# A transformer kernel on one core: splitting the first load, moving key preparation, and spreading the entering tiles' work over rounds and queues

## The chip, the cores and the metric

The kernel runs on one core of a Trainium2 chip. The core has five engines that run side by side, each in the order of its own instruction list: TensorE (PE, matrix products and transposes), VectorE (DVE), ScalarE (ACT), GpSimd (POOL) and SyncE (SP), which here only issues transfers. ScalarE and GpSimd issue transfers as well. The metric is the device time of one execution in microseconds, as the median of several runs; lower is better.

## The reference

The input x has 4 batches of 1024 rows and 256 features. Two blocks follow each other, each with an attention over a context and a network behind it; everything is fp32.

```python
x = x + _L0_xattn_ref(_layernorm(x), ctx, ctx, mask, ...)   # 16 heads, 64 masked context keys
x = x + _L0_ffn_ref(_layernorm(x), ...)     # self-attention, gate, norm, 8 experts
x = x + _L1_xattn_ref(_layernorm(x), ctx, ctx, ...)         # 16 heads, no mask
x = x + _L1_ffn_ref(_layernorm(x), ...)     # 8 experts, each takes its 512 best rows
```

`_L0_ffn_ref` is the largest part: queries, keys and values from the normalised rows, scores over all 1024 rows of a batch for 16 heads, scaled by a factor that comes from each query (`sigmoid(q . scale_w) * 2`), softmax, a sigmoid gate, a projection, a layer norm, then one of 8 experts for each row (the larger index of the two best), and a layer norm.

## The kernel before, in words

The 4096 rows are 32 tiles of 128 rows, 8 to a batch; all of x stays on the chip in `xres`. The stages stand one behind the other: cross-attention 0 (to about 260 us), self-attention (to 1307), routing and the experts of the first block (to 1540), cross-attention 1, and the last network.

**Cross-attention** (`cross_attention`, L295) works in rounds. In round r, a list `steps` names what is done, and for which tile: ("share", 5) means that in round r tile r - 5 gets its step `share`. The list also sets the order within the round. While a set `in_order` holds an engine, the instructions that are made through `matmul`, `on_dve`, `on_act`, `on_pool` or `on_sync` stay in program order on it; otherwise the scheduler places them. Before the first round stands `cross_keys` (L259): it loads the weights `xw` and makes the keys of the whole context, `k_t`. `prepare(b)` makes batch b's keys, values and limits (from the mask) in round b, ahead of the round's steps.

In the same rounds runs `beside` (L1447): in round 4 it calls `Entrance.prepare` (scaled query weights and other constants), and from round 27 on (`FIRST_IN`) it lets the 8 tiles of the first batch enter self-attention. The class `Enter` (L552) has the steps of an entering tile: `stats`, `norm`, `turn` (transpose), `keys`, `values`, `queries`, `scale`, `gain`, and `spread`. Keys and queries are split by `halves` (L547) on GpSimd into a rounded part and the rest, by two instructions (L549, L550), into the tiles `kst` and `qst`. `kst` has a single buffer, which holds two tiles. After each second tile `spread` (L610) issues eight transfers of 64 KB that lay these keys out for the heads in `k_rows` (L618). The Entrance also loads three rows (`gb_half`, `n1g`, `last`) by ScalarE's queue as soon as it is made.

**Self-attention** (L623) works in units of 512 queries and 4 heads. `Unit.spread` (L664) lays out a unit's queries by four transfers of 128 KB (L670); `first` makes scores to find each query's largest (`tops`, L694 on VectorE), `second` makes them again, and takes the exponential on ScalarE. The other batches' tiles enter during this stage, by `enter` (L638). The two pools of the stage, sa1 and sa2, take over the memory of pools that are closed by then; a pool without `reuse_waits="tile"` waits for all of what lay there, one with it only for the tiles that it overlaps.

**Routing and experts** (L976): from the counts of the routing, a chain of small VectorE instructions (all shown as L1007, the helper `v`) makes the list of slots, `slot_i` and `slot_row_i`. SyncE reads these (L1053, L1064) to choose the weights and the rows `x_s` that it loads (L1057, L1065). The second block's keys, `k_t` of layer 1, are made by `cross_keys` ahead of this chain, and the batches' keys and values by `meanwhile` behind it.

The instructions that the prediction names by line: L412 is `share`, L401 `lower`, L324 the limits, L392 and L393 `tops` of cross-attention, L408 and L409 `sums`, L442 `bias`, L445 `add`, L598 the tanh of `scale`, L603 `gain`, L269 the eviction of `k_t`. L123 and L126 are the helpers of all products and transposes.

Of the kernel before, what the change touches and what calls it, by code (L numbers as in the profile page):

```python
# [68 lines left out]
def two_blocks(  # L69
# [106 lines left out]
    nc.sync.dma_start(out=xres[:, 0:TB], in_=x_v[:, 0:TB])  # L176
# [20 lines left out]
    def on_all(pool, first, n, queue, width=D):  # L197

        at = ROWS.index(first) * D
        t = new(pool, [P, n, width], f"row_{first}")  # L200
        queue.dma_start(
            out=t.rearrange("p n d -> p (n d)"), in_=rows[at : at + n * width].partition_broadcast(P)
        )
        return [t[:, i] for i in range(n)]
# [54 lines left out]
    def cross_keys(one, layer, xw, queue):  # L259

        bk = cols_sb[:, 4 * layer + 2 : 4 * layer + 4]
# [3 lines left out]
        k_t = new(one, [P, 2, B * SK], f"k_t{layer}")  # L265
        for m in range(2):
            ps = bank()
            product(ps[:, : B * SK], ws[1][:, :, m * P : (m + 1) * P], ctx_sb)
            nc.vector.tensor_scalar(k_t[:, m], ps[:, : B * SK], bk[:, m : m + 1], None, ALU.add)  # L269
        return ws, k_t, *on_all(one, f"bo{layer}", 2, queue)  # L270
# [24 lines left out]
    def cross_attention(layer, ws, k_t, bo, bv, prepared=None, beside=None):  # L295
# [4 lines left out]
        with tc.tile_pool(name=f"xb{layer}", bufs=2) as work:  # L300
# [176 lines left out]
            for r in range(NT + last + (layer == 0)):  # L477
                if r < NT:
                    tiles_of[r] = Tile(r)
                if r < B:  # L480
                    prepare(r)
                for name, behind in steps:
                    if r - behind in tiles_of:
                        getattr(tiles_of[r - behind], name)()
                if beside is not None:
# [23 lines left out]
    class Entrance:  # L509


        def __init__(self, even, pool):
# [6 lines left out]
            self.gb_half = new(pool, [P, 2], "gb_half")  # L519
            at = ROWS.index("gb") * D  # L520
            nc.scalar.dma_start(out=self.gb_half, in_=rows[at : at + D].rearrange("(m p) -> p m", p=P))
            self.n1g, self.n1b = on_all(pool, "n1g", 2, nc.scalar)
            (self.moe_gb,) = on_all(pool, "last", 1, nc.scalar, E)
# [28 lines left out]
    class Enter:  # L552
# [22 lines left out]
        def keys(self):  # L575
            i = self.i
            if i % 2 == 0:
                self.b["kst"] = new(self.ent.pool, [P, 2, 2, 2 * P], "kst", F32R, bufs=1)
            k_f = new(self.work, [P, 2, P], "en_f", bufs=3)
            on_act(nc.scalar.copy(k_f, by_feature(w_k, self.xn_t)))  # L580
            halves(self.b["kst"][:, :, :, i % 2 * P : (i % 2 + 1) * P], k_f)
# [19 lines left out]
        def gain(self):  # L601
            th = self.th
            on_dve(nc.vector.scalar_tensor_tensor(th, th, 1.0, self.q_f, ALU.add, ALU.mult))  # L603
            self.b["gained"] += 1
# [3 lines left out]
            halves(self.b["q"][half][:, :, :, at : at + P], th)  # L608

        def spread(self):  # L610
# [3 lines left out]
            if i % 2 == 0:  # L614
                return
            for g in range(4):
                for half in range(2):
                    nc.sync.dma_start(  # L618
# [936 lines left out]
```

## Time and profile before

| | us |
|---|---|
| median of 3 runs | 2011.66 (2010.49 to 2013.72) |
| the profiled execution's own time | 2024.04 |
| its span | 2022.3 |
| PE busy | 1803.0 (89%) |
| DVE busy | 1409.4 (70%) |
| ACT busy | 1055.6 (52%) |
| POOL busy | 842.3 (42%) |

The busy shares are means over stages with different limits. The chain of waits goes back from the last instruction, at each step to what released it, so its shares say what the time was spent on. In the answers, "idle before" in brackets is the idle time of the engine ahead of an instruction, with what ended it. SPq and ACTq are transfers being issued by SyncE and ScalarE. A wait for several things is put down to the one that came last.

### The profile page before, as it was taken

Reading aid. Unit: us, or ns where it says so; the run is one execution under the profiler, and the core shown is the slowest. Engines: PE = TensorE matmul, PEld = TensorE weight load, DVE = VectorE, ACT = ScalarE, POOL = GpSimd, SP = SyncE. Lnnn points to the kernel's source line nnn. Section 1 sums busy time; section 2 is a strip of 40 time slices with the busy share of each in tenths; the row PEclk is TensorE's granted clock in tenths of the full one; section 3 lists DMA queues with packets and bytes.
Section 4 is the critical chain, followed back from the end, with each engine's and each line's share of the span. In section 5 each row is a group of like instructions: output and inputs, shape, how many; then the busy total and the mean of one; then the engine's idle time right before and its main releaser. Section 6 shows DMA issues by size and latency. Waiting matters only on the chain.

```text
span 2022.3 us, 36959 instructions
## 1 busy us (share of the span) xinstructions
PE 1803.0 (89%) x13599; PEld 1079.3 (53%) x13599; DVE 1409.4 (70%) x2970; ACT 1055.6 (52%) x2201; POOL 842.3 (42%) x1262
## 2 busy tenths in 40 slices
PE   6998779999999999999999999969996888837998
PEld 4666644355455454554544444446664666624566
DVE  6998477877777778777787878266775887854232
ACT  2666416666666666666666666613333666601111
POOL 4888531022232322222322202126667888704443
PEclk8999879999999999999999999979997999957999
DMA  9995120010110101110101100058883311103442
GB/s 276 223 224 119 28 63 22 22 33 22 32 33 22 43 22 26 34 27 22 43 19 51 33 17 1 11 189 253 258 276 95 123 62 57 57 11 84 109 97 36
DMA packets 143443, 160.62 MB, mean 79 GB/s; under 512 B 24976, under 2 KB 116624, under 8 KB 143264
## 3 DMA queue, kind: packets, MB, share of 16 engines
q1 hardware_dynamic: 123552, 128.33, 24.6%
q0 software_dynamic: 9216, 16.93, 3.7%
q10 hardware_dynamic: 10496, 13.01, 1.9%
q8 instruction: 108, 1.77, 0.4%
q14 instruction: 71, 0.58, 0.1%
HBM read 77.33 MB, written 55.72 MB: 66 GB/s over the span
## 4 chain that ended last, share of the span: by engine, by line
PE 62%; DVE 18%; POOL 10%; issue 4%; DMA 3%; ACT 1%; SPq 1%; another core or an unknown queue 0%; POOLq 0%; ACTq 0%; DVEq 0%
PE bank L123 35%; PE acc L123 12%; PE two_banks L123 8%; DVE tops L694 5%; PE bank L126 5%; POOL pr L412 3%; PE first L123 3%; POOL rstd L221 2%; DMA x_s<-xs_d 2%; DVE w_sum L408 2%; DVE mx L393 1%; DVE pr L392 1%; POOL y L248 1%; DVE bn_st L218 1%; DVE xres L442 1%
## 5 line engine op out<-in xcount | busy, mean ns | idle before, releaser
L694 DVE TENSOR_REDUCE tops<-first 128x1 f32<-128x512 f32 x1002 | 644.5, 684 | 218.6 <-PE first L123 180.1
L726 ACT ACTIVATE e<-bank 128x512 f32<-128x512 f32 x1024 | 555.3, 595 | 330.4 <-PE bank L123 309.4
L123 PE MATMUL first<-k_rows,q_rows 32*128 32x512 f32 x2004 | 412.3, 452 | 40.1 <-DVE tops L694 33.2
L123 PE MATMUL bank<-q_rows,k_rows 32*128 32x512 f32 x2048 | 408.8, 451 | 2.3 <-ACT e L726 1.9
L123 PEld LDWEIGHTS bank<-q_rows,k_rows 32*128 32x128 f32 x2048 | 175.6, 184 | 263.9 <-issue 136.5
L123 PE MATMUL acc<-e,vals 128*32 128x512 f32 x2048 | 285.6, 611 | 0.0
L123 PE MATMUL bank<-m_rows,ones_r 32*128 32x512 f32 x1024 | 220.4, 393 | 0.0
L123 PEld LDWEIGHTS first<-k_rows,q_rows 32*128 32x128 f32 x2004 | 169.6, 186 | 77.5 <-DVE tops L694 66.2
L220 POOL TENSOR_SCALAR rstd<-mv 128x1 f32<-128x1 f32 x206 | 49.8, 242 | 338.9 <-DVE mv L219 329.3
L412 POOL TENSOR_TENSOR pr<-pr,w_sum 128x1024 f32<-128x1024 f32 x64 | 126.3, 1974 | 8.2 <-DVE w_sum L409 6.3
L221 POOL TENSOR_TENSOR rstd<-rstd,mhalf 128x1 f32<-128x1 f32 x206 | 121.9, 592 | 17.2
L420 ACT COPY pr_t<-two_banks 128x1024 f32<-128x1024 f32 x64 | 64.8, 1012 | 118.0 <-PE two_banks L126 118.0
L123 PEld LDWEIGHTS bank<-m_rows,ones_r 32*128 32x128 f32 x1024 | 112.6, 185 | 14.1
L123 PE MATMUL two_banks<-xg_t,ew 128*128 128x512 f32 (+1 forms) x288 | 113.1, 551 | 0.0
L549 POOL CAST qst<-en_th 128x256 fp32r<-128x256 f32 x32 | 13.3, 417 | 215.3 <-DVE en_th L603 215.3
L126 PE MATMUL two_banks<-ident,pr 128*128 128x128 f32 x512 | 72.3, 286 | 29.2 <-POOL pr L412 28.9
L123 PEld LDWEIGHTS acc<-e,vals 128*32 128x32 f32 x2048 | 42.7, 108 | 102.1 <-issue 92.6
L1385 ACT ACTIVATE h_t<-two_banks 128x512 f32<-128x512 f32 (+1 forms) x36 | 19.8, 550 | 145.1 <-PE two_banks L123 145.1
L254 POOL DMA_INDIRECT out_x<-y,tok_i x32 | 50.4, 1574 | 98.9 <-DVE y L1213 91.9
L126 PEld LDWEIGHTS two_banks<-ident,pr 128*128 128x128 f32 x512 | 58.1, 145 | 51.2 <-POOL pr L412 50.1
L1386 DVE TENSOR_TENSOR h_t<-h_t,two_banks 128x512 f32<-128x512 f32 (+1 forms) x36 | 22.6, 628 | 89.1 <-ACT h_t L1385 84.3
L123 PE MATMUL bank<-xw,o_t 128*128 128x256 f32 x256 | 71.0, 400 | 14.1 <-ACT q_t L366 11.1
(287 smaller groups left out, 3413.5 us busy)
## 6 DMA issues: line engine op xcount, KB each, us to landing
w_s<-in_w SPq DMA_DIRECT2D x78, 512.0 KB, 5.3
xs_d<-zeros SPq DMA_DIRECT2D x8, 4112.0 KB, 53.2
q_rows<-qst SPq DMA_DIRECT2D x128, 128.0 KB, 2.4
k_rows<-kst SPq DMA_DIRECT2D x128, 64.0 KB, 2.0
ew<-in_e SPq DMA_DIRECT2D x15, 512.0 KB, 3.9
x_s<-xs_d SPq DMA_DIRECT2D x39, 128.5 KB, 4.1
ys_d<-y ACTq DMA_DIRECT2D x39, 128.0 KB, 3.5
ew<-in_e ACTq DMA_DIRECT2D x9, 512.0 KB, 5.8
```

The costliest lines, as they stand in the source:

```text
L123: return placed(nc.tensor, nc.tensor.matmul(*args, **kw))
L126: return placed(nc.tensor, nc.tensor.transpose(*args))
L218: on_dve(nc.vector.bn_stats(st, src))
L220: on_pool(nc.gpsimd.tensor_scalar(r, mv[:, 1:2], EPS, None, ALU.add))
L221: on_pool(nc.gpsimd.tensor_tensor(r, r, mhalf, ALU.pow))
L254: return nc.gpsimd.indirect_dma_start(out=dst[:], out_offset=bass.IndirectOffsetOnAxis(ap=idx, axis=0), in_=src[:], in_offset=None, comput ...
L408: on_dve(nc.vector.tensor_reduce(self.w, self.pr, AX.X, ALU.add))
L412: on_pool(nc.gpsimd.tensor_tensor(self.pr, self.pr, self.w.unsqueeze(2).to_broadcast(bc), ALU.mult))
L420: on_act(nc.scalar.copy(self.pr_t.rearrange("p j q -> p (j q)"), tp))
L694: nc.vector.tensor_reduce(self.part[:, i, j, at : at + 1], self.ps[j], AX.X, ALU.max)
L726: nc.scalar.activation(self.es[k][:, j], ps, AF.Exp)
L1386: on_dve(nc.vector.tensor_tensor(h, h, ps[:, CAP : CAP + n], ALU.mult))
```

## The change

1. The load of the first batch of x is issued in two parts, tiles 0 and 1, then 2 to 7.
2. `cross_keys` is divided: `cross_weights` loads, and a new `cross_keys` makes `k_t`, with its eviction in VectorE's program order. For layer 0 it is called in round 0 behind the steps. For layer 1 it is called in `meanwhile`, behind the chain that makes the slots.
3. `prepare(r)` is called behind the steps of its round. The Entrance's three row loads are issued in round 2 (in ScalarE's order), and `Entrance.prepare` runs in round 6.
4. For the tiles of the first batch, the key split and `spread` come one round later than the keys, and the query split one round later than `gain`; the key copy has buffers of its own (`en_k`). The cross-attention has one more round for this.
5. Of the last pair's eight key transfers, four are issued by SyncE and four by ScalarE. The first unit's four query transfers are issued by ScalarE.
6. The pools sa1 and sa2 get `reuse_waits="tile"`.

On the engines the lists stay the same but for these moves: TensorE's order differs only by the batches' value products in the first rounds.

```diff
-    nc.sync.dma_start(out=xres[:, 0:TB], in_=x_v[:, 0:TB])
+    for first, end in (0, 2), (2, TB):
+        nc.sync.dma_start(out=xres[:, first:end], in_=x_v[:, first:end])
...
-    def cross_keys(one, layer, xw, queue):
-
-        bk = cols_sb[:, 4 * layer + 2 : 4 * layer + 4]
+    def cross_weights(one, layer, xw, queue):
+
         w = new(one, [P, 2, 4 * D], f"xw{layer}")
         queue.dma_start(out=w, in_=xw.rearrange("(c p) n -> p c n", p=P))
         ws = [w[:, :, i * D : (i + 1) * D] for i in range(4)]
-        k_t = new(one, [P, 2, B * SK], f"k_t{layer}")
+        return ws, new(one, [P, 2, B * SK], f"k_t{layer}"), *on_all(one, f"bo{layer}", 2, queue)
+
+    def cross_keys(layer, ws, k_t):
+        bk = cols_sb[:, 4 * layer + 2 : 4 * layer + 4]
         for m in range(2):
             ps = bank()
             product(ps[:, : B * SK], ws[1][:, :, m * P : (m + 1) * P], ctx_sb)
-            nc.vector.tensor_scalar(k_t[:, m], ps[:, : B * SK], bk[:, m : m + 1], None, ALU.add)
-        return ws, k_t, *on_all(one, f"bo{layer}", 2, queue)
+            on_dve(nc.vector.tensor_scalar(k_t[:, m], ps[:, : B * SK], bk[:, m : m + 1], None, ALU.add))
...
-            for r in range(NT + last + (layer == 0)):
+            for r in range(NT + last + 2 * (layer == 0)):
                 if r < NT:
                     tiles_of[r] = Tile(r)
-                if r < B:
-                    prepare(r)
                 for name, behind in steps:
                     if r - behind in tiles_of:
                         getattr(tiles_of[r - behind], name)()
+                if r == 0 and layer == 0:
+                    cross_keys(0, ws, k_t)
+                if r < B:
+                    prepare(r)
...
         def keys(self):
+            self.k_f = new(self.work, [P, 2, P], "en_k" if self.on_scalar else "en_f", bufs=2 if self.on_scalar else 3)
+            on_act(nc.scalar.copy(self.k_f, by_feature(w_k, self.xn_t)))
+
+        def split_keys(self):
             i = self.i
             if i % 2 == 0:
                 self.b["kst"] = new(self.ent.pool, [P, 2, 2, 2 * P], "kst", F32R, bufs=1)
-            k_f = new(self.work, [P, 2, P], "en_f", bufs=3)
-            on_act(nc.scalar.copy(k_f, by_feature(w_k, self.xn_t)))
-            halves(self.b["kst"][:, :, :, i % 2 * P : (i % 2 + 1) * P], k_f)
+            halves(self.b["kst"][:, :, :, i % 2 * P : (i % 2 + 1) * P], self.k_f)
...
+            queues = (nc.sync, nc.scalar) if self.on_scalar and i == TB - 1 else (nc.sync, nc.sync)
             for g in range(4):
                 for half in range(2):
-                    nc.sync.dma_start(
+                    placed(
+                        queues[half],
+                        queues[half].dma_start(
...
-        with tc.tile_pool(name="sa1", bufs=1) as one, tc.tile_pool(name="sa2", bufs=2) as work:
+        with (
+            tc.tile_pool(name="sa1", bufs=1, reuse_waits="tile") as one,
+            tc.tile_pool(name="sa2", bufs=2, reuse_waits="tile") as work,
+        ):
...
+                    queue = nc.scalar if self.first_of_all else nc.sync
                     for half in range(2):
                         for r in range(2):
-                            nc.sync.dma_start(
+                            queue.dma_start(
...
-            enter_steps += ("spread", 3), ("scale", 4), ("gain", 4)
+
+            enter_steps += ("scale", 4), ("gain", 4), ("split_keys", 4), ("spread", 4), ("split_queries", 5)
 
             def beside(work, r):
 
-                if r == 4:
+                if r == 2:
+                    ent.load()
+                if r == 6:
                     ent.prepare()
...
     def meanwhile():
+        cross_keys(1, *keys_1[:2])
         prepared.extend(keys_of_batch(xa1, 1, *keys_1[:2], keys_1[3], b) for b in range(B))
```

`ent.load` is the new home of the three row loads (in ScalarE's order); `split_queries` holds the two lines of `gain` that took the query split.

## The prediction

> **What bounds the kernel now.** I read the page first, then the chain of waits by windows, then the timeline at the three places that the edit touches: the first 45 us, the end of the first cross-attention (190 to 265 us), and the step from self-attention to the routed layer (1325 to 1345 us).
>
> ```profile
> span 2022.3 us, 36959 instructions
> PE 62%; DVE 18%; POOL 10%; issue 4%; DMA 3%; ACT 1%; SPq 1%; another core or an unknown queue 0%; POOLq 0%; ACTq 0%; DVEq 0%
> ```
>
> TensorE carries 62% of the chain, but none of the edited places is limited by TensorE: there the chain is on VectorE, GpSimd, SyncE's queue and loads. So a microsecond saved at these places is a microsecond of the span, as long as what follows is in series. It is: self-attention can't start before all keys of the first batch have landed, and the routed layer can't before routing.
>
> Start, from the timeline (start, duration, what, and in brackets the idle time before it):
>
> ```profile
> 16.07 1.28 ACT L350 ACT_TABLE_LOAD   x1 [16.07 <-DMA row_n1g<-in_rows]
> ...
> 19.51 0.69 PE L126 MATMUL bank<-ident,xn 128*128 128x128 f32 x2 [3.38 <-ACT xn L350]
> 20.00 0.43 DVE L324 TENSOR_SCALAR lim<-lim 128x512 f32<-128x512 int32 x1 [0.30 <-DMA lim<-in_mask]
> ...
> 29.15 1.22 DVE L392 TENSOR_TENSOR pr<-two_banks,lim 128x1024 f32<-128x1024 f32 x1
> ```
>
> ScalarE does nothing until 16.07, because three row loads (gb_half, n1g, last) stand in its queue. VectorE, from 45 to 165 us the busiest engine (117.75 of 120 us), does its first score row at 29.15.
>
> The ring of the entering tiles, from the chain of waits (start, duration, what):
>
> ```profile
> 213.59 1.09 PE two_banks L126 x8
> 214.68 1.06 PE two_banks L123 x8
> 215.74 0.37 PE bank L126 x2
> 216.11 3.11 PE bank L123 x24
> ...
> 220.63 0.74 POOL qst L550
> 221.37 1.87 POOL pr L412
> ...
> 253.58 0.74 POOL kst L550
> ...
> 260.60 2.46 DMA q_rows<-qst
> ...
> 263.19 0.76 PE first L123
> ```
>
> Read the first six as a circle: the shares (L412) feed the transposes, these are followed in TensorE's order by the entering tile's products; tanh, gain and the first half of the query split (219.25 to 220.56) are left out; its second half (L550) stands before the next L412 in GpSimd's order. L412 starts at 192.13, 201.94, 211.63, 221.32, 231.29, 241.45: 9.7 to 10.2 us a round, against 5.6 us before. The last three show the exit: key split done at 254.32, then 12 issues in SyncE's queue (8 keys, 4 queries), the last starting at 260.60, and its landing.
>
> Routing, from the timeline:
>
> ```profile
> 1330.85 0.48 DVE L269 TENSOR_SCALAR k_t<-bank,cols_sb 128x256 f32<-128x256 f32 x1 [1.21 <-PE bank L123]
> ...
> 1332.53 0.48 DVE L269 TENSOR_SCALAR k_t<-bank,cols_sb 128x256 f32<-128x256 f32 x1 [1.20 <-PE bank L123]
> 1332.93 0.16 DVE L1007 TENSOR_TENSOR total<-next_row,region 128x8 f32<-128x8 f32 x1
> ```
>
> VectorE ends place_i at 1329.63 and then waits for TensorE's layer 1 keys, while the routing (total, and from it slot_i, for which SyncE's queue waits) stands behind.
>
> **The change part by part.** The sum is made on the profiled execution: span 2022.3, its own time 2024.04, which is 12.4 above the median of 2011.66. I take the difference over to the median unscaled, since the edited stretches are short.
>
> *Start.* Two issues instead of one for x (0.44 us each on SyncE, which waits for its own loads anyway) let tile 0 arrive with a quarter of the bytes. Its statistics move ahead of the keys, and the masks' and keys' preparation of each batch behind the round's steps. Tile 0's chain then ends when GpSimd's setup does (12.4) plus rstd, power, shift, xn (0.31+0.61+0.26+0.60 with gaps: 15.0), and the transposes follow the first values' product at about 15.0 instead of 19.51. The following rounds do the same VectorE work: keys, values, limits 2.2 us, statistics 0.6. Limits of batch 1 still wait for a load (20.00 before, perhaps 19.4 with 256 KB of n1g gone from ahead). Counted on from there: limits 1 end at 20.4, statistics 2 at 21, batch 2 at 24, tops of tile 0 start at 24.6 (29.15 before); but batch 3's 2.2 us now lie behind these, so that tops of tile 1 start at 29.7 against 32.10. That is 2.4 us, kept by a VectorE that is full from there on. The scaling of w_q and its two neighbours (4 us on VectorE) moves from round 4 to 6, paid in both. The three row loads cost ScalarE 0.37+0.35+0.35 us at round 2; the transfers before them in its queue are over by then. Ends: 0.5 us, if limits 2 and 3 are as late as the loads let them be; 4.6, if all of the 29.15 to 24.6 is kept. I take 2.4, since the 2.2 us of batch 3 are paid anyhow.
>
> *Entering.* Key split, key transfers and query split go one round later, so the ring opens. What is late next is a longer circle: gain (VectorE), the next round's tops 2.45, sums with reciprocal 1.46, bias and add about 1.6, statistics 0.6, then GpSimd's rs 1.3, both splits 2.26, L412 1.9. Counted on by these rows, with L412 at 184.54 unchanged, the next start at 191.0 (no key split in that round), 198.8, 210.5, 219.0 and 228.5. The last of these in full: TensorE's transposes after 210.5 + 1.9, its products 5.55 (1.07+0.37+3.11 and the transposes' 1.0), tanh and gain 0.85 end at 218.8; + 2.45 + 1.46 + 1.6 + 0.6 on VectorE is 224.9, + 1.3 + 2.26 on GpSimd is 228.5. Then comes a new wait: there is one buffer for two tiles' split keys, so a pair's first split waits for the previous pair's landings. Pair 1's split ends at 227.4, its last issue starts 7 x 0.635 later (231.8) and lands after 2.0: 233.9. GpSimd waits there, and shares, lower and everything behind it with it. Two splits 2.26: L412 of the last tile at 236.2, against 241.45. So of the 9.7 us rounds only 5.2 us are won in five. At the end the same wait returns: pair 2's split ends at 239.2, lands at 245.8, then key, query, key splits (3.4) end at 249.3 against 254.32.
>
> *Two queues.* The last eight key transfers go four and four; ScalarE then issues the four queries. But ScalarE is in order, and ahead stand the last two tanh. The last follows TensorE's last keys by 3.4 us, as before (252.56 to 255.97): 251.0 if TensorE runs the last rounds as now, 249.5 at full clock. Eight issues, seven intervals of 0.635, then 2.46 to landing and 0.14: TensorE's first complete products at 258.0 or 256.5 against 263.19. So entering and queues together give 5.2 to 6.7; I take 5.5, nearer the present clock (0.83 in the rounds of 221 to 251 us). The other queries' issues stay on SyncE and come earlier; ScalarE's next work, a copy at 277.34, is far. The lifted pool waits (reuse by tile) hide behind these transfers: GpSimd's memset waited for the query split until 258.21, but what needs it comes in the next batch; without this cover they would be worth no more than the 0.6 us from 258.15 to 258.74. Ends for this part: 1.5 (only the issues saved less the wait for tanh) and 9.
>
> The Trainium skill's page "DMA: Bandwidth & Descriptors", section "Issuing engines are not separate DMA queues", speaks against the two queues: all queues run on the same 16 engines, and a second issuing engine saves only the sequencer's time, "usually small relative to the DMA itself". The rows show 12 issues taking 7.6 us against 2.46 for a landing, so here the small part is the large one. Were the page right on the size, this part would give under 1 us and the sum would be about 10 instead of 11.2.
>
> *Routing.* The two k_t evictions go behind the routing's chain on VectorE (pos ends at 1341.95 before), so total starts at 1329.65 instead of 1332.93: 3.3 us earlier, and slot_i, SyncE's loads and x_s with it. In the way: the scatters into xs_d (last issue ends 1335.47; transfers run to about 1337) are over when x_s would now be issued (1337.2). TensorE's last two value products wait for the evictions' banks (1339.6) and end about 1340.6, before slot 0's transposes (1344.45 - 3.3 = 1341.1). The evictions' 0.96 us delay the layer 1 keys, which are needed in 200 us. Ends: 1.0 (scatters or banks hold x_s) and 3.3. I take 3.3.
>
> Sum: 2.4 + 5.5 + 3.3 = 11.2 us. 2011.66 - 11.2 = 2000.5 (profiled: 2024.0 - 11.2 = 2012.8).
>
> **The rivals.**
> 1. *All three as summed*: 2000.5, with 1992.7 (4.6+9+3.3, and 2 for the clock) to 2006. For it: each of the waits is printed with its releaser.
> 2. *The key buffer takes the place of the ring.* If landing takes a microsecond or two longer than the 2.0 measured, the wait on pairs 1 and 2 eats the 5.2 us and the entering gives 1.5. Then 2011.66 - 2.4 - 1.5 - 3.3 = 2004.5. For it: the wait is really added; against: DMA share is 0.06 to 0.16 in these rounds.
> 3. *Hidden anyway.* The start stays at the pace of its loads (0.5), x_s waits for scatters (1.0), entering 1.5: 3.0 us, 2008.7, which is within 0.2%.
> 4. *Slower: the wait on landings becomes the bound.* GpSimd now waits three times (pairs 0, 1, 2) for eight landings with the whole softmax queued behind. The far row is the load of x at 12.4 us to landing: three times 10.4 more gives 2000.5 + 31 = 2031.7. It decides from 5 us more each (11.2 + 4 = 15). Against it: the queues are nearly empty there.
>
> **How the numbers follow.** Chances: 0.62, 0.18, 0.11, 0.09. 0.2% (4 us) is about what a measurement of this kernel can tell from no change. Cases 1 and 2 are faster (0.80), with 0.01 of case 3 above the bound; case 3 leaves 0.10 as the same; case 4 0.09 slower. Predicted is case 1. The range reaches over cases 1 to 3: below to 1992.7, the sum of the upper ends (17) with 2 for a half-clock spell of 3.4 us more or less; above to 2009.
>
> **What would show it.** Right: the first table load of ScalarE near 4 us, the first tops near 24.6; L412 of the last tile near 234 (236 less the start's 2.4), the key splits of tiles 4 and 6 released by a DMA; eight issues between the last tanh and the first products, these about 8 us earlier in the span; total directly after place_i, and slot 0's transposes 11 us earlier. Wrong: an L412 period still near 9.7 with no DMA wait, ScalarE held at its three row loads at round 2, or slot 0 waiting for scatters.

## The result, and the profile after

The changed kernel takes 2008.63 us against 2014.57 us for the kernel before (medians of 19 runs each on the same chip); the ratio is 0.9975 with a 95% interval of 0.9967 to 0.9983, which is 5.0 us less (3.4 to 6.6). The forecast was 11.2 us less. The time lay inside the range given, but less than half of the gain came.

The profiled execution of the changed kernel took 2008.63 us, its span is 2006.9. The profiled execution of before, on which the prediction was built, took 2024.04, which is 9.5 above the median of its 19 runs: from the first score row of self-attention to the start of the last place_i (the routing's result, where each row goes) it needs 1065.5 us, and 1052.6 to 1059.1 in the sixteen other profiles of this case, with and without the change; why is not known. So the two spans must not be subtracted; the places are compared one by one. The page's chain of waits reaches back over the last tenth of the span only and then breaks off:

```profile
span 2006.9 us, 36970 instructions
...
PE 9%; DVE 2%; issue 1%; POOL 0%; DMA 0%; POOLq 0%; ACT 0%; ACTq 0%; DVEq 0%
```

So all that follows is read from timelines. In this kernel's lines L417 is `share`, L406 `lower`, L397 `tops`, L282 the keys and L293 the clearing of the values' buffer, L275 the eviction of `k_t`, L558 and L559 the splits, L609 the tanh.

The start, from the timeline of the changed kernel (start, duration, what, idle time before it):

```profile
4.82 1.28 ACT L355 ACT_TABLE_LOAD   x1 [4.82 <-DMA ctx_sb<-in_ctx_t]
...
25.42 1.23 DVE L397 TENSOR_TENSOR pr<-two_banks,lim 128x1024 f32<-128x1024 f32 x1
...
27.81 2.45 DVE L282 TENSOR_TENSOR keys<-k_t,head 128x256 f32<-128x256 f32 x2
...
27.98 2.01 POOL L406 TENSOR_TENSOR pr<-pr,mx 128x1024 f32<-128x1024 f32 x1 [1.28 <-DVE mx L398]
...
32.36 1.23 DVE L397 TENSOR_TENSOR pr<-two_banks,lim 128x1024 f32<-128x1024 f32 x1
```

ScalarE is free at 4.82 instead of 16.07, and the first tops start at 25.42 instead of 29.15, both near the forecast. But the two keys of batch 3, 0.73 us in the other rounds, now run while GpSimd works on `lower`, and take 2.45. Tile 1's tops start at 32.36; they started at 32.10 before. Nothing is left of the lead. The same place in the timeline of before, where L277 are the keys, L392 `tops`, and L526 and L527 are of `Entrance.prepare`:

```profile
25.12 0.72 DVE L277 TENSOR_TENSOR keys<-k_t,head 128x256 f32<-128x256 f32 x2
...
32.10 1.19 DVE L392 TENSOR_TENSOR pr<-two_banks,lim 128x1024 f32<-128x1024 f32 x1
...
36.75 1.94 POOL L526 MEMSET vals<- 128x2208 f32 x1
37.01 1.95 DVE L527 TENSOR_SCALAR wq<-fw_sb 128x512 f32<-128x512 f32 x1
```

The last two lines stood in the profile from which the prediction was made: a 128x512 `tensor_scalar`, which takes 0.43 us for the limits, took 1.95 beside a `memset` of GpSimd. The prediction counted it in its "4 us on VectorE" without asking why it was so long.

The last rounds of the entering tiles and the exit, from the same timeline:

```profile
229.28 1.90 POOL L417 TENSOR_TENSOR pr<-pr,w_sum 128x1024 f32<-128x1024 f32 x1
...
234.26 0.40 POOL L558 CAST kst<-en_k 128x256 fp32r<-128x256 f32 x1 [3.07 <-ACT en_x_t L239]
...
236.56 1.91 POOL L417 TENSOR_TENSOR pr<-pr,w_sum 128x1024 f32<-128x1024 f32 x1
...
245.73 0.40 POOL L558 CAST kst<-en_k 128x256 fp32r<-128x256 f32 x1 [4.76 <-DMA k_rows<-kst]
...
248.50 0.73 POOL L559 TENSOR_TENSOR kst<-en_k,kst 128x256 fp32r<-128x256 f32 x1
...
249.91 0.38 ACT L609 ACTIVATE en_th<-bank 128x256 f32<-128x256 f32 x1 [0.33 <-PE bank L123]
249.99 2.46 ACTq L635 DMA_DIRECT2D k_rows<-kst  x4
...
252.49 2.57 ACTq L694 DMA_DIRECT2D q_rows<-qst  x4
...
257.83 0.76 PE L123 MATMUL first<-k_rows,q_rows 32*128 32x512 f32 x1 [0.87 <-DMA q_rows<-qst]
```

All of this is as forecast: shares at 229.28 and 236.56 (forecast 228.5 and 236.2), GpSimd's two new waits for the key buffer, key splits done at 249.23 (249.3), then the last tanh, eight issues of ScalarE, and the first complete products at 257.83 instead of 263.19. (The first of the two waits is put down to ScalarE's `en_x_t`, which came last. That it was the key buffer shows in the kernel with two of them, below: there the wait is gone.)

Routing, from the same timeline, and the row of SyncE's waits there (engine, line, what it waited for: us in total, times, longest):

```profile
1314.01 0.17 DVE L902 CAST place_i<-place 128x4 int32<-128x4 f32 x1
1314.09 0.16 DVE L1031 TENSOR_TENSOR total<-next_row,region 128x8 f32<-128x8 f32 x1
...
1317.69 3.26 SPq L1081 DMA_DIRECT2D w_s<-in_w  x3
...
1319.06 1.18 POOL L258 DMA_INDIRECT xs_d<-xr,place_i  x1 [0.30 <-issue]
...
1323.55 2.73 PE L123 MATMUL bank<-xw,ctx_sb 128*64 128x256 f32 x16 [4.16 <-DVE k_t L275]
...
1324.39 0.36 SPq L1089 DMA_DIRECT2D x_s<-xs_d  x1
...
1326.66 0.66 PE L126 MATMUL bank<-ident,x_s 128*128 128x128 f32 x2 [0.38 <-DMA x_s<-xs_d]
```

```profile
SPq L1089 <- DMA xs_d<-xr,place_i: 2.4, 2, 1.3
```

The same in the timeline of before, where place_i starts at 1329.46:

```profile
1336.61 2.81 SPq L1057 DMA_DIRECT2D w_s<-in_w  x3
...
1340.49 0.36 SPq L1065 DMA_DIRECT2D x_s<-xs_d  x1
...
1344.45 0.66 PE L126 MATMUL bank<-ident,x_s 128*128 128x128 f32 x2 [8.31 <-DMA x_s<-xs_d]
```

`total` follows place_i directly, as forecast, and the first weights are issued 3.5 us earlier after place_i (3.7 us instead of 7.2). But `x_s` is issued 10.4 us after the start of place_i, against 11.0 before: SyncE waits 2.4 us in all for the scatters to land. And TensorE's values products wait 4.16 us for the evictions.

### The profile page after: what moved, and what is told of

It is laid out like the page before. It is cut to its first block, busy times and chain, and to the rows that moved or that the text cites. A ratio compares the mean times of both kernels' runs of the same rounds, so it can differ in the third digit from the quotient of the medians.

```text
span 2006.9 us, 36970 instructions
## 1 busy us (share of the span) xinstructions
PE 1795.7 (89%) x13599; PEld 1071.9 (53%) x13599; DVE 1412.4 (70%) x2970; ACT 1055.0 (53%) x2201; POOL 842.8 (42%) x1262
## 5 line engine op out<-in xcount | busy, mean ns | idle before, releaser
L417 POOL TENSOR_TENSOR pr<-pr,w_sum 128x1024 f32<-128x1024 f32 x64 | 126.5, 1976 | 8.3 <-DVE w_sum L414 6.3
L558 POOL CAST qst<-en_th 128x256 fp32r<-128x256 f32 x32 | 13.4, 418 | 208.1 <-DVE en_th L614 208.1
L1410 DVE TENSOR_TENSOR h_t<-h_t,two_banks 128x512 f32<-128x512 f32 (+1 forms) x36 | 22.6, 628 | 89.9 <-ACT h_t L1409 89.9
L222 DVE BATCH_NORM_STATS2 bn_st<-xres 128x6 f32<-128x256 f32 x128 | 53.3, 416 | 43.5 <-POOL xres L345 43.2
L123 PEld LDWEIGHTS two_banks<-xg_t,ew 128*128 128x128 f32 x288 | 55.0, 193 | 54.0 <-issue 50.9
```

What stands on the lines that cost most here:

```text
L123: return placed(nc.tensor, nc.tensor.matmul(*args, **kw))
L222: on_dve(nc.vector.bn_stats(st, src))
L417: on_pool(nc.gpsimd.tensor_tensor(self.pr, self.pr, self.w.unsqueeze(2).to_broadcast(bc), ALU.mult))
L1410: on_dve(nc.vector.tensor_tensor(h, h, ps[:, CAP : CAP + n], ALU.mult))
```

## The experiments

Each entry's time is the ratio to the kernel before, timed on the same chip, turned into microseconds of its median. Times after place_i count from the start of its last instruction.

### One part undone at a time

The start put back:

```
- for first, end in (0, 2), (2, TB): load x
+ load x[:, 0:TB]
- if r == 0 and layer == 0: cross_keys(0, ...)      # before the loop again
- if r < B: prepare(r)                              # ahead of the steps again
- if r == 2: ent.load()                             # when Entrance is made
- if r == 6: ent.prepare()
+ if r == 4: ent.prepare()
```

> The changed kernel with its start put back (x in one load, the first layer's keys before the loop, each batch's preparation ahead of the round's steps, ScalarE's three row loads at the beginning, the scaling of w_q at round 4). Theory A, the lead of the first tile is used up again by tile 1 (keys of batch 3 take 2.45 us beside GpSimd's lower instead of 0.73, and the values' memset stands behind it) and by round 6: the share of tile 24 or so at 163.4 as in both profiles, and the time equals the changed kernel's, 5.0 us below before (3.4 to 6.6). Theory B, the start is worth its 2.4 us and something later takes them: 2.6 us below before, and the shares 2.4 us later than the changed kernel's.

5.8 us below before (2.8 to 8.9), against 5.0 for the changed kernel. Tile 1's tops start at 32.58, and the share that stands at 163.41 in the changed kernel at 163.89, 0.5 later (in the kernel before it stands at 163.44). By the rows this is theory A: the start as changed is worth 0.5 us at most. Theory B's 2.6 us below before lies only just outside the interval of the time.

All of the exit on SyncE's queue:

```
- queues = (nc.sync, nc.scalar) if self.on_scalar and i == TB - 1 else (nc.sync, nc.sync)
+ queues = (nc.sync, nc.sync)
- queue = nc.scalar if self.first_of_all else nc.sync
+ queue = nc.sync
```

> The changed kernel with all twelve transfers of the exit on SyncE's queue. By the rows of the changed kernel: key splits end at 249.2, twelve issues of 0.635 start at 249.3, the last at 256.3, landing 2.46 later, first complete products at 258.9 instead of 257.83. Theory A, most of the gain there comes from the steps and not from the second queue, because ScalarE is held by the last tanh until 249.9: about 1.1 us slower than the changed kernel, 3.9 below before. Theory B, the second queue carries the gain: 4 us slower, 1 below before.

4.8 us below before (2.4 to 7.1), so 0.2 from the changed kernel. From the end of the last key split to the first complete products it takes 8.84 us here, and 8.60 in the changed kernel. Even theory A's 1.1 us was too much. The issues show why: the last of the first unit's four query issues starts 5.20 us after the last key split in the changed kernel and 6.29 here, 1.1 us apart as theory A has it. But from this issue to the first complete products it takes 3.40 us in the changed kernel and 2.55 here. It is the same in all profiles: 2.95 to 3.50 us in the fourteen with two queues, 2.55 to 2.59 in the three with SyncE's queue alone. With two queues SyncE issues the next unit's queries meanwhile; that these transfers are what delays the landing was not tried.

The splits back in their rounds:

```
- ("scale", 4), ("gain", 4), ("split_keys", 4), ("spread", 4), ("split_queries", 5)
+ ("split_keys", 3), ("values", 3), ("queries", 3), ("spread", 3), ("scale", 4), ("gain", 4), ("split_queries", 4)
```

> The changed kernel with key split and key transfers back in the round of the products, and the query split back in the round of the gain; two queues kept. Theory A (the entering is the whole gain at this place): shares 9.7 to 10.2 us apart again, key splits end near 254.3, last tanh 256.0, eight issues on ScalarE's queue, first complete products near 263.0; 5.2 us slower than the changed kernel, so about equal to before. Theory B (the ring's gain is mostly taken by the waits for the single key buffer, and the queues give the rest): 2 to 3 us slower than the changed kernel.

1.2 us below before (-1.2 to 3.6): the entering steps carry most of what the change gains. The shares are 9.0 to 10.2 us apart again. The timeline of this kernel shows a cost of the second queue too, when it stands at a bad place:

```profile
255.95 2.45 ACTq L635 DMA_DIRECT2D k_rows<-kst  x4
258.44 0.38 ACT L609 ACTIVATE en_th<-bank 128x256 f32<-128x256 f32 x1 [2.18 <-DMA k_rows<-kst]
...
263.84 0.76 PE L123 MATMUL first<-k_rows,q_rows 32*128 32x512 f32 x1 [0.69 <-DMA q_rows<-qst]
```

With the old steps the key transfers come ahead of the last two tanh in ScalarE's order and hold them until 258.44.

The routing's move undone:

```
- def meanwhile(): cross_keys(1, ...)
+ keys_1 = cross_weights(...); cross_keys(1, ...)    # ahead of the chain
```

> The changed kernel with the second layer's key products evicted ahead of the routing's chain again. Theory A (x_s waits for the scatters, which now share the DMA engines with the first weights, and the value products wait for the evictions): slot 0's transposes 2.4 us later after place_i than in the changed kernel, time 2.5 us above it, 2.5 below before. Theory B (the routing kept its 3.3): 3.3 us above the changed kernel. Theory C (given back in the slots): equal to the changed kernel.

6.4 us below before (3.2 to 9.7): not slower than the changed kernel. Slot 0's transposes are 2.4 us later after place_i (15.09), but the last slot's stand at 195.3 against 194.1, and from place_i to the end it takes 691.3 us against 692.9. Theory C: the interval excludes the 2.5 and 1.7 us below before of theories A and B.

### What holds the start

Batch 3's preparation ahead of round 3's steps, as it was before:

```
+ if r == B - 1: prepare(r)
  for name, behind in steps: ...
- if r < B: prepare(r)
+ if r < B - 1: prepare(r)
```

> The changed kernel with batch 3's keys, values and limits ahead of round 3's steps, so that its keys don't run beside GpSimd's lower of tile 0; batches 0 to 2 as changed. Theory A (the start's lead was eaten by that collision): the keys take 0.73 us again instead of 2.45, tops of tile 1 start near 30.6 instead of 32.36, the share at 163.41 comes 1.7 us earlier, and the time is 1.7 us below the changed kernel's. Theory B (the start is held by its loads or by the round with the scaling of w_q whatever VectorE does): shares at 163.4 unchanged, time equal to the changed kernel's.

The keys take 0.75 us again, and still this kernel's timeline of VectorE gives:

```profile
27.74 0.43 DVE L329 TENSOR_SCALAR lim<-lim 128x512 f32<-128x512 int32 x1 [1.81 <-DMA lim<-in_mask]
...
29.21 1.23 DVE L397 TENSOR_TENSOR pr<-two_banks,lim 128x1024 f32<-128x1024 f32 x1
...
32.16 1.19 DVE L397 TENSOR_TENSOR pr<-two_banks,lim 128x1024 f32<-128x1024 f32 x1
```

Now the limits wait 1.81 us for the mask of batch 3, which lands at 27.7. The share moves by 0.2 us only: the profile speaks for theory B. The time is 8.5 us below before (5.6 to 11.3, five runs), 3.5 more than the changed kernel's, for which no row was found. Between kernels of different groups, a difference of 3 us in the times should not be trusted without rows.

Only the keys and values of batch 3 ahead, the limits behind:

```
+ if r == B - 1: prepare(r)      # keys, values
  steps
+ if r < B: limits(r)
```

> The changed kernel with only the keys and values of batch 3 ahead of round 3's steps, and its limits behind them. Theory A (two things each take the start's lead alone: behind the steps the keys collide with GpSimd's lower, ahead of them the limits wait for the mask's load until 27.7): neither acts here, tops of tile 0 near 26.4, tops of tile 1 near 30.2 instead of 32.36, the share at 163.41 comes 2.0 us earlier and so does the end. Theory B (VectorE's rounds to 52 us take any lead): the share within 0.3 us of 163.4.

This kernel's timeline of the place:

```profile
26.84 1.22 DVE L397 TENSOR_TENSOR pr<-two_banks,lim 128x1024 f32<-128x1024 f32 x1
...
29.41 2.10 POOL L406 TENSOR_TENSOR pr<-pr,mx 128x1024 f32<-128x1024 f32 x1 [1.29 <-DVE mx L398]
...
29.78 2.00 DVE L331 TENSOR_SCALAR lim<-lim 128x512 f32<-128x512 f32 x1
...
32.26 1.19 DVE L397 TENSOR_TENSOR pr<-two_banks,lim 128x1024 f32<-128x1024 f32 x1
```

The limits collide with `lower` as the keys did: 2.00 us instead of 0.43. Tile 1's tops are at 32.26 once more; 5.8 us below before (3.2 to 8.5). Theory A had said that neither obstacle acts here; the first was only passed on to another instruction.

The values' buffers cleared in round 0, on top of that:

```
+ for i in range(B): cleared[i] = new(...); on_pool(nc.gpsimd.memset(cleared[i], 0.0))   # in round 0
```

> The kernel of the last entry, with the four values' buffers cleared by GpSimd in round 0 instead of one in each round behind rstd and shift, where VectorE's values wait for it (1.06 us in rounds 1 and 2 in every profile so far). Theory A: 2.1 us more, tops of tile 0 near 24.3, tops of tile 1 near 28.1, the share at 163.41 comes 4 us earlier. Theory B: TensorE's values products or GpSimd's rstd take its place, under 0.5 us more than the last entry.

5.4 us below before (2.8 to 7.9). The two waits of 1.06 us go, but one of 2.14 for TensorE's values products comes, the limits again take 2.00, and the first layer's weights land at 11.9: tops at 33.32. Theory B.

The same without the routing's move:

```
- def meanwhile(): cross_keys(1, ...)
+ cross_keys(1, ...)             # ahead of the chain
```

> The kernel with batch 3's keys ahead and the buffers cleared in round 0, but without the routing's move: entering, queues and the mended start. If the start keeps 4 us and the routing is worth nothing: as fast as the kernel of entry c2, some 9 us below before. If the routing is worth 2.4 us: 2.4 slower than that one.

5.4 us below before (2.6 to 8.1), the same as with the move. Its start keeps nothing either (tops at 33.19, weights at 11.8).

So the obstacles were taken away together, with all masks loaded ahead of the later batches of x:

```
  for b in range(B): load mask b
+ for b in range(1, B): load x of batch b
+ if r == B - 1: prepare(r)      # ahead of the steps, as in the first kernel of this group
```

> The changed kernel with all four masks loaded ahead of the last three batches of x, and all of batch 3's preparation ahead of round 3's steps, so that neither the mask's load (1.81 us) nor the collision with lower (1.72 us) acts. Theory A (the lead exists and these two took it): batch 3 done near 27.0, tops of tile 0 near 27.4, tops of tile 1 near 30.4 instead of 32.36, the share of 163.41 131.0 us after that, at 161.4, and 1.9 us below the changed kernel at the end. Theory B (something else holds the rounds until 32): tops of tile 1 at 32.1 or later.

The timeline of VectorE in this kernel:

```profile
24.86 0.76 DVE L282 TENSOR_TENSOR keys<-k_t,head 128x256 f32<-128x256 f32 x2
...
26.25 0.43 DVE L329 TENSOR_SCALAR lim<-lim 128x512 f32<-128x512 int32 x1
...
27.72 1.22 DVE L397 TENSOR_TENSOR pr<-two_banks,lim 128x1024 f32<-128x1024 f32 x1
...
30.66 1.19 DVE L397 TENSOR_TENSOR pr<-two_banks,lim 128x1024 f32<-128x1024 f32 x1
```

No wait, no collision: tops at 30.66 (expected 30.4), the share at 161.74 (161.4), 8.9 us below before (5.0 to 12.9). The lead exists, and two obstacles each took it alone.

```
- for first, end in (0, 2), (2, TB): load x
+ load x[:, 0:TB]
```

> The same with x's first batch in one load again. Theory A (the second issue delays the first layer's weights): weights land at 9.9 instead of 10.5 to 11.9, everything up to tops of tile 1 0.6 to 2 us earlier than in the last entry. Theory B (tile 0's statistics need the early quarter): statistics of tile 0 later than 12.6 and tops later by as much.

11.9 us below before (8.1 to 15.9); weights at 9.81, tops at 30.23, the share at 161.30, statistics of tile 0 no later. This is theory A for the weights (0.9 us earlier), but only 0.4 of it reaches tile 1's tops, less than the 0.6 that theory A named. And with the cleared buffers:

```
+ cleared[i] for all batches in round 0
```

> The same as d2 with the four values' buffers cleared in round 0, ahead of the rounds' rstd and shift. Theory A: the waits of 1.06 us in rounds 1 and 2 go and tops of tile 1 come 2.1 us earlier than in d2, near 28; 4 us below the changed kernel. Theory B: TensorE's values products (2.14 us waited for in the entry with the cleared buffers) take their place, under 0.7 us more than d2.

13.1 us below before (9.3 to 16.7; ratio 0.9935, 0.9917 to 0.9954), tops at 29.79: 0.4 more by the rows, theory B, as one wait of 1.40 us for TensorE's values takes the place of the clearing's two. This is the fastest kernel of the study; the interval of its ratio lies below that of the changed kernel, though the two were timed against different runs of before. The rows of the start explain 2.6 us of the 8 us between the two; the rest was not found in a row and stays open.

The start in one table (us). The fourth column is the share that stands at 163.41 in the changed kernel.

| kernel | first product of the layer's weights | in the way | tile 1's tops | that share | distance |
|---|---|---|---|---|---|
| before | 9.85 | its order | 32.10 | 163.44 | 131.34 |
| start put back | 9.90 | its order | 32.58 | 163.89 | 131.31 |
| changed | 10.66 | keys beside lower, 2.45 | 32.36 | 163.41 | 131.05 |
| batch 3 first | 10.51 | mask's load, 1.81 | 32.16 | 163.23 | 131.07 |
| keys 3 ahead | 10.66 | limits beside lower, 2.00 | 32.26 | 163.02 | 130.76 |
| masks first | 10.72 | nothing of these | 30.66 | 161.74 | 131.08 |
| and x in one | 9.81 | nothing of these | 30.23 | 161.30 | 131.07 |
| and cleared | 9.88 | nothing of these | 29.79 | 160.82 | 131.03 |
| all three repairs (below) | 11.70 | mask's load, 2.45 | 34.67 | 165.72 | 131.05 |

The last column shows that a lead at tile 1's tops is carried on for 131 us, to within 0.6 us. The 4 us of `Entrance.prepare` in round 6 instead of 4, which looked in the timeline as if they ate the lead, eat nothing.

### The key buffer

```
- self.b["kst"] = new(self.ent.pool, ..., "kst", F32R, bufs=1)
+ pairs 1 and 3: new(xa0, ..., "kst_1", F32R, bufs=1)      # pairs 0 and 2 as before
```

> The changed kernel with a second buffer for split keys (pairs 0 and 2 in one, pairs 1 and 3 in the other), so that no split waits for the landing of the pair before. Theory A (the two waits of GpSimd, 3.07 and 4.76 us, are on the path): last share near 233.5 instead of 236.56, key splits end near 246 instead of 249.23, first complete products near 255 instead of 257.83, 2.5 us below the changed kernel. Theory B (they are beside other work: ScalarE's last tanh at 249.9 holds the exit): key splits earlier, but the first complete products within 0.7 us of 257.83, and the time equal.

6.2 us below before (3.2 to 9.3), not told apart from the changed kernel. The wait ahead of the last share goes (4.1 us from share to share instead of 7.3), but the exit stands, as this kernel's timeline shows:

```profile
252.46 0.38 ACT L611 ACTIVATE en_th<-bank 128x256 f32<-128x256 f32 x1 [0.33 <-PE bank L123]
...
255.08 2.56 ACTq L696 DMA_DIRECT2D q_rows<-qst  x4
...
259.99 0.76 PE L123 MATMUL first<-k_rows,q_rows 32*128 32x512 f32 x1 [0.61 <-DMA q_rows<-qst]
```

The last tanh, behind TensorE's last products, sets when ScalarE issues. This profile belongs to those with a half-clock spell in these rounds (next section), so the fair comparison is with such profiles of one buffer: from the share of the table above to the first complete products it is 96.3 us here, and 96.2 in the kernel with keys 3 ahead and cleared buffers, though the last share comes 2.8 us sooner here. Theory B: the new waits were beside the path.

### The entering steps, over all profiles

From the share of the table above to the end of the last key split the profiles give 85.82 (changed) and 90.87 (before). But the move of the routing alone, whose entering is that of before, has 88.52. The windows of three kernels tell the difference (stretch; its length, busy time of PE, PEld, DVE, ACT and POOL with instructions; granted clock; DMA share; GB/s). Before:

```profile
211.60:231.30 19.70, 15.30 (x119) 12.54 (x117) 11.92 (x18) 9.64 (x20) 14.05 (x20) 0.91 0.11 27
231.30:252.60 21.30, 16.52 (x118) 14.88 (x118) 4.16 (x8) 6.81 (x15) 8.24 (x11) 0.84 0.10 25
```

The routing's move alone:

```profile
213.20:231.90 18.70, 14.04 (x119) 10.97 (x117) 12.69 (x18) 9.47 (x20) 13.96 (x19) 1.00 0.11 29
231.90:251.60 19.70, 14.78 (x117) 13.18 (x118) 4.22 (x8) 6.63 (x15) 8.29 (x11) 0.91 0.11 27
```

The changed kernel:

```profile
211.00:229.30 18.30, 13.66 (x117) 10.92 (x116) 12.70 (x18) 9.04 (x19) 14.25 (x20) 1.00 0.12 30
229.30:249.00 19.70, 16.66 (x132) 14.97 (x132) 4.66 (x8) 7.77 (x18) 11.31 (x17) 0.91 0.20 51
```

Before's profile ran these rounds at a granted clock of 0.91 and 0.84, the other two at 1.00 and 0.91. The profiles of the same entering differ in this: of the fourteen with the new entering, seven give 85.8 to 86.2 us and seven 87.3 to 88.3. Two rounds, from share to share, show the difference. The changed kernel:

```profile
211.07:219.71 8.64, 6.19 (x58) 5.16 (x58) 5.41 (x8) 3.65 (x9) 6.97 (x10) 1.00 0.21 53
219.71:229.28 9.57, 7.45 (x58) 5.76 (x58) 7.20 (x11) 5.37 (x11) 7.19 (x10) 1.00 0.03 9
```

Keys 3 ahead and cleared buffers:

```profile
211.75:220.38 8.63, 6.67 (x39) 5.61 (x40) 4.86 (x7) 2.63 (x5) 6.96 (x10) 0.80 0.21 53
220.38:231.99 11.61, 8.38 (x80) 6.60 (x78) 9.04 (x14) 6.49 (x13) 7.19 (x11) 1.00 0.03 8
```

In six of the seven longer profiles the first of these rounds has a clock of 0.80, and the second takes 11.5 to 11.7 us; in the other eight the first has 1.00, and the second takes 9.6.

The mean of the fourteen is 86.8; the mean of the three with the old entering is 89.9 (88.5 to 90.9). So the steps are worth about 3.1 us, not the 5.1 by which the first two profiles differ there; with three profiles on one side this is good to about 1 us. From the end of the key split to the first complete products, the mean of the thirteen profiles with the new entering and two queues is 8.59 us, and 8.84 to 8.88 in the three kernels with SyncE's queue alone: the second queue is worth 0.3 us.

Part 6 of the change, the pools' waits, was undone in no run. Up to the first complete products it shows nothing: with SyncE's queue alone that stretch is 8.84 and 8.88 us with the old pools and 8.84 with the new.

### The routing

The move alone, on the kernel before:

```
- cross_keys ahead of the chain makes k_t of layer 1
+ meanwhile makes it, behind the chain, its evictions in VectorE's order
```

> The kernel before with only the second layer's key products and their evictions moved behind the routing's chain. Theory A (the routing keeps what its first slot shows): slot 0's transposes 1.5 to 2.4 us earlier after place_i than the 15.0 of before, and 2.4 us less time. Theory C (the slots take it back): slot 3 within 0.7 us of 26.6 after place_i, and the time within 1 us of before.

0.8 us below before (-1.2 to 3.0). Slot 0's transposes come 13.27 after place_i instead of 15.0, slot 3's at 25.22 instead of 26.6, and the last slot's at 195.87 against 196.64. By time theory C fits, and the interval still holds theory A's 2.4; by rows neither does: slot 3 keeps 1.4 us, more than C allowed, and the last slot 0.8, less than A.

The evictions by ScalarE, and slot 0's rows ahead of the weights of slots 1 and 2:

```
- on_dve(nc.vector.tensor_scalar(k_t[:, m], ps, bk, None, ALU.add))
+ nc.scalar.activation(k_t[:, m], ps, AF.Identity, bias=bk)       # layer 1
+ if len(slots_of) == 1: slots_of[0].load()
```

> The changed kernel with the second layer's key products evicted by ScalarE, and slot 0's rows, second weights and norms issued between the first weights of slot 0 and of slot 1. Theory A (the head start of the routing is lost to the scatters behind the first weights and to the eviction's banks, and is kept if these go): x_s issued near 7.8 us after the end of place_i instead of 10.2, slot 0's transposes near 10.2 instead of 12.5, and 2.4 us below the changed kernel at the end. Theory C (the slots take a head start back, since their first ones run at the pace of their weight loads and at half the clock): slot 0 earlier by 2.4, but slot 8 at 47.4 to 49.3 as in all profiles so far, and the time equal to the changed kernel's.

4.8 us below before (1.8 to 7.7), as the changed kernel. TensorE's values products no longer wait, but `x_s` is issued at 9.66, not 7.8, for SyncE still waits 3.7 us for the scatters; slot 0 is at 11.95, slot 1 at 20.2 (its weights are later now) and slot 8 at 50.0, later even than theory C's 47.4 to 49.3. Theory C.

| after place_i | old order (3 profiles) | moved (12 profiles), mean and range |
|---|---|---|
| x_s issued | 11.03 to 11.04 | 10.64 (10.36 to 11.16) |
| slot 0's transposes | 14.99 to 15.41 | 13.22 (12.65 to 13.61) |
| slot 3's | 26.43 to 26.74 | 25.56 (24.63 to 27.07) |
| last slot's | 195.1 to 196.6 | 194.9 (191.6 to 198.0) |
| end of the span | 691.3 to 693.4 | 692.0 (687.7 to 694.0) |

The forecast gave 3.3 us to x_s and to all that follows. It is 0.4 at x_s, 1.9 at slot 0, 1.0 at slot 3, and at the end 0.5 between means, within the scatter of single profiles. The reason at x_s is in the transfers: GpSimd's last scatter issue ends 6.0 to 6.3 us after place_i in all of them, but the scatters' last packet starts 7.1 to 7.2 us after place_i in the old order (before, and with the move undone), 9.8 in the changed kernel and 9.9 with the move alone, where the three first weights (512 KB each) are already under way, and 8.5 where only one is. The chain that comes earlier starts the weights earlier, and these push back the scatters that `x_s` needs. Why slots 1 to 3 take back the half of slot 0's lead was not settled; in the trials the first slots ran at the pace of their loads, with TensorE waiting for `x_s` at slots 1 to 3 by 0.3 to 3.4 us in several profiles.

### All three repairs at once

```
+ batch 3 first, two key buffers, slot 0's rows early
```

> All three edits (batch 3's preparation first, two key buffers, slot 0's rows early with ScalarE's evictions) on the changed kernel. If each were kept: 1.7 + 2.5 + 2.4 = 6.6 us below the changed kernel, some 11.6 below before. If the slots take theirs back: 4.2 below the changed kernel. If all three are hidden: equal to it.

5.0 us below before (2.8 to 7.1), as the changed kernel. This does not show that three gains are hidden: in its profile the start is not mended but 2.3 us later (the share at 165.72), as the first weights come at 11.70 and the limits of batch 3 wait 2.45 us for their mask; the exit is that of the two key buffers alone, and slot 8 stands at 51.1 us after place_i, later than in any other profile.

## Where the prediction held and where it failed

**The start, 2.4 us: failed.** The step "batch 3's 2.2 us now lie behind these, so that tops of tile 1 start at 29.7" took the durations from rows where GpSimd ran nothing long. Behind the first tops GpSimd runs `lower`, and the keys took 2.45 us instead of 0.73, with the first product of the layer 0.8 us later besides. The lower end of this term (0.5) named the loads as the thing that could hold it; that is what holds it when the order is put right (1.81 us for a mask). The measured term is 0 to 0.5 us by the rows, and by time it can't be told from 0. The Trainium skill has the rule that should have been applied: its page "SBUF — State Buffer", section "Who interferes with whom", says that a VectorE instruction with two inputs in SBUF contends with a GpSimd instruction that reads SBUF, that the shared port is held for a whole instruction, and that `tensor_scalar` can contend too. The rows 2.45 (two tensors) and 2.00 (`tensor_scalar`), each beside a `lower` of 2.0 to 2.1 us, agree with it.

**Entering and two queues, 5.5 us: the mechanism was right, the size was not.** Every row of the new circle came as worked out (shares within 0.8 us of the forecast, key splits at 249.23 for 249.3, products at 257.83 for 256.5 to 258.0). The term was mis-sized because it was measured against one profile of before whose rounds ran at 0.91 and 0.84 of the clock: against all profiles it is about 3.1 us for the steps and 0.3 for the queues. The predicted wait on the single key buffer came, at both places, but beside the path: rival 2 falls, and so does rival 4, as the waits are 3.07 and 4.76 us.

**The rule on the queues was right in its conclusion.** The prediction weighed a sentence of the skill's page "DMA: Bandwidth & Descriptors", section "Issuing engines are not separate DMA queues", that a second engine saves only the issuing time, against the 7.6 us that 12 issues took, and kept the larger number. By the rows the issuing is not small beside a landing of 2.46 us, so the page's reason does not fit here; its conclusion does. ScalarE's issues can't start before its last tanh at 249.9, and then eight take 5.0 us; and the step "then 2.46 to landing and 0.14" failed, since 3.40 us passed from the last issue to the first complete products. The second queue saved 0.3 us, less than the 1 us that the prediction gave to the rule.

**Routing, 3.3 us: failed.** The step "the scatters into xs_d are over when x_s would now be issued" read the scatters' landing off a profile in which the weights came later. They are part of what moves: the last packet starts at 9.8 us after place_i, not at 7.1. The prediction's own sign of being wrong, slot 0 waiting for scatters, came. This was rival 3's mechanism (x_s waits for the scatters); it had a price of 2.3 us (3.3 to 1.0), and by the rows more was lost: 0.4 us is left at x_s and 0.5 at the end. By time the move alone gives 0.8 us (-1.2 to 3.0). The second thing named as being in the way, the values products that wait for the evictions' banks, came as well (4.16 us).

**The rivals.** Rival 3 (hidden anyway) named the start and the scatters rightly and the entering wrongly; the result lies between it and rival 2. With 0.62 on all three parts, the prediction gave far too much to the case that three separate waits, once removed, leave nothing behind.

Sum by rows: 0 + 3.1 + 0.3 + 0.5 to 0.8 is 3.9 to 4.2 us, in the measured 3.4 to 6.6. Each of these terms is known to about 1 us at best.

## What to carry to other kernels

Before costing moved work by its duration, look at what the other engines will be doing at the new place: an instruction that took 0.43 us cost 2.00 beside GpSimd, and a transfer that was early ended 2.7 us later once the loads behind it had been pulled forward too. Two obstacles that each hold the same place look like no gain when either is removed alone; remove both before giving an idea up. And measure a stretch in several profiles before and after: a term read from one pair was wrong here by 2 of 5 us, and a single round with the granted clock at 0.80 moves the same stretch by 2 us.

## What the runs showed of the hardware

- VectorE's 128x512 `tensor_scalar` in SBUF took 2.00 us beside a GpSimd `tensor_tensor` of 2.10, 1.95 beside a GpSimd `memset` of 1.94, and 0.43 without either; two 128x256 `tensor_tensor` took 2.45 beside a GpSimd `tensor_tensor` of 2.01, instead of 0.73.
- With the 1 MB of x in two issues (256 and 768 KB), the first layer's weights, loaded by ScalarE's queue, were used from 9.94 to 12.85 us (mean 11.0 in twelve profiles); with x in one issue from 9.81 to 9.97 (five profiles). What lies behind it was not tried.
- From the last of four query issues (128 KB each) to the products that need them it took 2.95 to 3.50 us when ScalarE issued them while SyncE issued others (fourteen profiles), and 2.55 to 2.59 when SyncE issued all in order (three).
- Four scatters by GpSimd, whose last issue ends 6.0 to 6.3 us after place_i, had their last packet start at 7.1 to 7.2 us with no weights loading, at 8.5 with one load of 512 KB issued ahead, and at 8.9 to 10.4 with three (twelve profiles).
- In the trace's clock records the granted clock fell to half for spells of 3.4 us, or a few times that, in rounds where TensorE waits a few microseconds in each; which rounds it hit differed from run to run, and it moved the same stretch of the same work by 2 us (85.8 to 86.2 us against 87.3 to 88.3).
